# Four graph-attention layers on one core: buffer counts of three tiles, and the order and queues of the first loads

## The chip, the core and the metric

The kernel runs on one core of one Trainium2 chip. The core has a matrix engine (TensorE, PE in the profile), a vector engine (VectorE, DVE), an activation engine (ScalarE, ACT), a general engine (GpSimd, POOL), and SyncE (SP), which here only starts transfers. Each engine works through its own part of the program in the order written, and engines wait for one another on semaphores. Transfers are carried by 16 DMA engines that all issuers share. The metric is the time on the device in microseconds (us); the median over several executions is compared.

## What is computed

The input is 64 graphs ("groups" in the kernel) of 256 nodes with 256 features in float32, and for each an int32 adjacency matrix of 256 by 256. Four attention layers follow one another, each with a residual and a layer norm. The part around the change is the beginning of layer 0:

```python
q = proj(Wq, bq)
k = proj(Wk, bk)
v = proj(Wv, bv)
attn = jnp.einsum('bhnd,bhmd->bhnm', q, k) * scale
attn = jnp.where(adj[:, None, :, :] == 0, NEG, attn)
attn = jax.nn.softmax(attn, axis=-1)
out = jnp.einsum('bhnm,bhmd->bhnd', attn, v)
...
out = out @ Wo.T + bo
...
x = _layernorm(x + _L0_gnn_ref(...), axis=-1)
```

Layer 1 has eight heads whose queries, keys and values are the normed rows themselves, and an MLP of width 1024; layer 2 is additive attention; layer 3 is dot-product attention with edge types. All matrix products are float32.

## The kernel before

`usual_input` (lines 450 to 1171) writes out the program for all 64 groups. Each group is seven generators, called threads: `a` (load, mask, q, k, v, attention of layer 0), `u` (its normalization, output projection, norm), `z` (a transposition), `b` (attention of layer 1), `w`, `c` (MLP), `o` (the rest). Every `yield` ends a step. The order in which steps of different groups are written is laid down by hand: `FIRST` lists the first 657 steps as pairs of a thread letter and a group, `PLACES` gives the places within the steady period, `LAST` lists the end. The class `InOrder` (line 466) ties each engine's instructions to exactly this order; nothing is reordered later. Because every operation passes through it, nearly all lines of the profile carry its line, L475, and are told apart by tile names.

Steps that matter here, for a group g:

- `a`, step 0: `load_edges(g)` starts the transfer of the adjacency matrix into `adj` (2 buffers). Step 1 (line 720): ScalarE converts it to bfloat16, `adjb`, and squares it in place to check it. Step 2 (line 724): two transposing transfers on SP make `adjT` from `adjb`. Step 3: `load_x(g)`, four transfers into `turned` and one into `x` (for group 0 only the latter). Step 4: VectorE makes `xT`. Step 5 (line 741): VectorE makes `mask` from `adjT` and `adjb`; after it both are free. Then the matrix products for q, k, v and scores `ps`, the exponential `e` on ScalarE, its product with the mask on VectorE, sums `ea`, and the product of `e` with `v` on PE.
- `u` (line 806): VectorE takes the reciprocals of the softmax sums (`few`, `back`), then step 1 writes them to DRAM (`lines`), step 2 reads them back with two transfers, spread over 128 partitions, into `rr` (line 825), and step 3 (line 834) multiplies `oT` by `rr` on VectorE. After that `rr` is free. Step 4 is the product with `Wo`.
- `z`: `put` writes `z` to DRAM as `rows`, `get` reads it back as `blk`, VectorE turns it to `t`, ScalarE scales `t`, and the scores of layer 1 (`ps<-t` on PE) follow.

`BUFS` (line 46) gives the number of buffers of each tile name. When a tile has no free buffer, the first instruction that writes the next one waits until the last reader of the old one is done. Before the change `rr` has 2, `adjb` and `adjT` have 1 each.

At a few places in `FIRST` two groups are close together. Counting the steps of `FIRST` from 0, group 3's `rr` is read from DRAM at step 191 and used at 206; group 4's is read at 208 and used at 209. Group 2's `put` of `z` is step 220.

The weights' first loads are lines 570 to 578; the others are queued in `later` and started from SP step by step. `load` (line 537) takes the engine whose queue starts the transfer.

Of the kernel before, what the change touches and what calls it, by code (L numbers as in the profile page):

```python
# [18 lines left out]
D = 256  # L19
# [23 lines left out]
WARM = 2  # L43
XQ = True
DIRECT = {0: ('x', 'z', 'o', 'yT'), 63: ('yT', 'n2', 'n3', 'o')}
BUFS = {'t': 7, 'q': 3, 'k': 1, 'v': 3, 'y': 4, 'z': 4, 'xb': 4, 'both': 2, 'xn': 6, 'mask': 9, 'e': 7, 'x0': 3, 'turned': 2, 'blk': 4, 'oT': 3, 'zs': 1, 'rr': 2, 'xT': 1, 'qT': 1, 'kT': 1, 'adj': 2, 'adjb': 1, 'adjT': 1, 'hT': 2, 'ea': 3}
PLACES = {
# [402 lines left out]
def usual_input(ctx: ExitStack, tc: tile.TileContext, a: dict, out: bass.AP, flag: bass.AP):  # L450
# [34 lines left out]
    PE, DVE, ACT, POOL, SP = (InOrder(e) for e in (nc.tensor, nc.vector, nc.scalar, nc.gpsimd, nc.sync))  # L485
    matmul, transpose = PE.matmul, PE.transpose

    def new(pool, shape, dtype, name, bufs=None, tag=None):
        tag = tag or name
        if bufs is None:  # L490
            bufs = BUFS.get(tag)
        t = pool.tile(shape, dtype, name=name, tag=tag, **({} if bufs is None else dict(bufs=bufs)))
        return t
# [22 lines left out]
    def load_edges(g):  # L516
        adj = new(io, [P, TB, N], I32, "adj")
        SP.dma_start(adj, a["adj"][g].rearrange("(q p) k -> p q k", p=P))
        return adj

    def load_x(g):
        turned = None
        if FX and "x" not in DIRECT.get(g, ()):
            turned = new(io, [P, NC, N // 32, 32], F32, "turned")
            parts = a["x"][g].rearrange("(t i) (c k j) -> k i c t j", i=32, c=NC, j=32)
            for k in range(P // 32):
                if XQ:
                    SP.dma_start(turned[32 * k:32 * k + 32], parts[k])
                for c in range(0 if XQ else NC):
                    SP.dma_start(turned[32 * k:32 * k + 32, c], parts[k, :, c])  # L530
        x0 = new(io, [P, TB, D], F32, "x0")
        SP.dma_start(x0, a["x"][g].rearrange("(q p) d -> p q d", p=P))
        return x0, turned
# [3 lines left out]
    def load(queue, to, of):  # L537
        if queue:
            queue.dma_start(to, of)
        else:  # L540
            later[-1].append((to, of))

    def load_rows(name, cols, queue=None, parts=1):

        src = a[name]
        n = src.shape[0] // P
        t = const.tile([P, n, cols], F32, name=name)
        of = src.rearrange("(c p) f -> p c f", p=P)
        for k in range(parts):
            if k:  # L550
                later.append([])
            some = slice(k * n // parts, (k + 1) * n // parts)
            load(queue, t[:, some], of[:, some])
        return t

    def load_column(src, n, name, queue=None):

        t = const.tile([P, n // P], F32, name=name)
        load(queue, t, src.rearrange("(c p) -> p c", p=P))
        return t  # L560
# [3 lines left out]
    def load_all(src, name, at=None, queue=None):  # L564

        t = const.tile([P, D], F32, name=name) if at is None else setup[:, at:at + D]
        load(queue, t, src.unsqueeze(0).to_broadcast([P, D]))
        return t

    ACT.activation(few_out[:, 0:1], minus_half, AF.Exp)  # L570
    x_first = load_x(0)
    wqT = load_rows("L0_gnn_WqT", D, SP)
    wkT = load_rows("L0_gnn_WkT", D, SP)
    first = load_edges(0), x_first
    bq = load_column(a["L0_gnn_bq"], D, "bq", POOL)
    bk = load_column(a["L0_gnn_bk"], D, "bk", POOL)
    wvT = load_rows("L0_gnn_WvT", D, ACT)
    beta0 = load_all(a["L0_gnn_beta"], "beta0", queue=ACT)
    later.append([])
    woT = load_rows("L0_gnn_WoT", D)  # L580
    bv = load_column(a["L0_gnn_bv"], D, "bv")
# [592 lines left out]
@with_exitstack  # L1174
def four_layers(ctx: ExitStack, tc: tile.TileContext, a: dict, out: bass.AP):
    nc = tc.nc
    keep = ctx.enter_context(tc.tile_pool(name="keep", bufs=1))
    flag = keep.tile([1, 1], I32, name="flag")
    usual_input(tc, a, out, flag)
    unusual = nc.values_load(flag)  # L1180
    with tc.If(unusual > 0):
        any_input(tc, a, out)
# [25 lines left out]
```

## Time and profile before

| | us |
|---|---|
| median of 3 executions (2369.64 to 2371.6) | 2371.16 |
| the profiled execution, its own time | 2374.09 |
| span of its trace | 2372.3 |
| PE busy in that span | 2338.2 (99%) |
| VectorE busy | 1924.6 (81%) |
| ScalarE busy | 1819.8 (77%) |
| GpSimd busy | 686.9 (29%) |

All starts given below are microseconds from the start of the span. A timeline line has the start, the time taken, the engine, the instruction, what it writes and reads, how many of them stand in the row, and in brackets the idle time before with what ended it. "SPq", "ACTq" mean the issue of a transfer by that engine's queue, not the transfer itself. A line of the chain of waits has the start, the time and what the end of the kernel was waiting for in it. A window line has the stretch, its length, the busy time of PE, its clock as granted (1.00 is full speed), the share of the DMA engines' time that is busy, and the rate.

### The profile page before, as it was taken

To read this page: it belongs to the slowest core of one execution; us is meant where nothing else is said; L and a number is where in the kernel's file an instruction comes from. 1 tells how busy PE (TensorE), PEld (TensorE's weight loads), DVE (VectorE), ACT (ScalarE), POOL (GpSimd) and SP (SyncE) were. 2 spreads that over 40 slices of the span, in tenths; PEclk is the share of its full clock that TensorE was granted. 3 is DMA by queue.
4 is the path that set the end of the run, shared out by engine and by line. 5 is a ranking of instruction groups with operands and counts; after the bars stand their busy time and mean duration, and the time that the engine had idled before them with its cause. 6 is when DMAs were issued, how large, how long until landed. Compare 5 with 4: busy or idle time off the path is not lost.

```text
span 2372.3 us, 50135 instructions
## 1 busy us (share of the span) xinstructions
PE 2338.2 (99%) x16124; PEld 1882.1 (79%) x16124; DVE 1924.6 (81%) x6175; ACT 1819.8 (77%) x3976; POOL 686.9 (29%) x1742
## 2 busy tenths in 40 slices
PE   8999999999999999999999999999999999999997
PEld 5677788788788788788788887887887887877786
DVE  5898888888878878878888888888788788778764
ACT  5677877778787788788777777787877887777766
POOL 1122323322332332223223223223323232323232
PEclk9999999999999999999999999999999999999999
DMA  5455555555555555555555555555545545455442
GB/s 129 103 113 118 109 117 112 110 117 116 110 120 111 115 120 112 117 116 110 123 112 107 121 113 111 118 112 112 121 111 116 119 110 120 103 109 116 90 86 68
DMA packets 1088884, 265.08 MB, mean 112 GB/s; under 512 B 859364, under 2 KB 1088232, under 8 KB 1088616
## 3 DMA queue, kind: packets, MB, share of 16 engines
q1 hardware_dynamic: 1088136, 261.42, 51.3%
q8 instruction: 130, 2.13, 0.4%
q14 instruction: 138, 1.13, 0.2%
q10 hardware_dynamic: 416, 0.39, 0.1%
q0 software_dynamic: 64, 0.00, 0.0%
HBM read 153.37 MB, written 99.88 MB: 107 GB/s over the span
## 4 chain that ended last, share of the span: by engine, by line
PE 90%; DMA 3%; ACT 2%; DVE 2%; SPq 2%; issue 1%; POOL 1%; DVEq 0%; ACTq 0%; POOLq 0%
PE pm L475 80%; PE ps L475 10%; SPq L475 2%; DMA blk<-rows 1%; ACT xn L475 1%; DMA rows<-z 1%; DMA turned<-in_x 0%; ACT e L475 0%; DMA adj<-in_adj 0%; DVE y L475 0%; ACT z L475 0%; POOL rstd L475 0%; DMA rr<-lines 0%; DVE e L475 0%; DVE xT L475 0%
## 5 line engine op out<-in xcount | busy, mean ns | idle before, releaser
L475 DVE SCALAR_TENSOR_TENSOR e<-e,mask 128x256 f32<-128x256 f32 x1024 | 368.8, 420 | 210.9 <-ACT e L475 210.8
L475 PE MATMUL pm<-t,L_gnn_W 128*128 128x256 f32 x2048 | 459.7, 382 | 0.4 <-ACT oT L475 0.4
L475 PE MATMUL pm<-L_gnn_W,hT 128*128 128x256 f32 (+1 forms) x2064 | 455.0, 380 | 0.1
L475 PEld LDWEIGHTS pm<-t,L_gnn_W 128*128 128x128 f32 x2048 | 384.5, 190 | 67.4 <-issue 16.1
L475 PEld LDWEIGHTS pm<-L_gnn_W,hT 128*128 128x128 f32 (+1 forms) x2064 | 389.2, 189 | 54.6 <-issue 1.7
L475 ACT ACTIVATE e<-ps 128x1024 f32<-128x1024 f32 x384 | 381.1, 1018 | 51.4 <-PE ps L475 50.7
L475 POOL TENSOR_TENSOR rstd<-ve,mhalf 128x2 f32<-128x2 f32 (+1 forms) x384 | 314.4, 819 | 32.0
L475 POOL TENSOR_SCALAR ve<-sq 128x2 f32<-128x2 f32 x256 | 75.4, 294 | 798.1 <-ACT xn L475 526.8
L475 POOL TENSOR_SCALAR ve<-mv 128x2 f32<-128x2 f32 x192 | 48.1, 251 | 784.5 <-DVE rz L475 462.1
L475 DVE STREAM_TRANSPOSE t<-blk 128x512 f32<-128x512 f32 x313 | 219.6, 704 | 16.7 <-DMA blk<-rows 16.1
L475 ACT ACTIVATE hT<-pm,b 128x256 f32<-128x256 f32 x512 | 201.2, 474 | 17.3 <-PE pm L475 16.5
L475 ACT ACT_TABLE_LOAD x127 | 162.9, 1283 | 2.4 <-PEq L1194 0.7
L475 DVE TENSOR_TENSOR e<-e,mask 128x1024 f32<-128x1024 f32 x128 | 150.9, 1218 | 11.6 <-ACT e L475 11.5
L475 PE MATMUL ps<-t 32*128 32x256 f32 x2048 | 151.1, 404 | 5.2 <-ACT t L475 4.1
L475 ACT ACTIVATE xn<-y,nm,rstd 128x256 f32<-128x256 f32 x256 | 138.5, 593 | 11.0 <-POOL nm L475 9.0
L475 ACT ACTIVATE xn<-y,sums 128x256 f32<-128x256 f32 x256 | 126.6, 497 | 18.2 <-DVE y L475 18.0
L475 PEld LDWEIGHTS ps<-t 32*128 32x128 f32 x2048 | 95.5, 186 | 56.5 <-ACT oT L475 19.7
L475 ACT ACTIVATE few_out<-few 128x8 f32<-128x8 f32 x64 | 13.3, 208 | 162.2 <-DVE few L475 162.1
L475 POOL TENSOR_SCALAR nm<-nm 128x2 f32<-128x2 f32 x320 | 128.9, 403 | 28.0
L475 PE MATMUL pm<-xn,q 128*128 128x257 f32 x512 | 130.9, 381 | 3.5 <-ACT q L475 3.4
L475 DVE SCALAR_TENSOR_TENSOR y<-pm,r,xn 128x256 f32<-128x256 f32 x256 | 123.9, 484 | 9.6
L475 PE MATMUL pm<-e,v 128*32 128x256 f32 x2048 | 124.0, 383 | 5.0 <-DVE e L475 4.6
(149 smaller groups left out, 4646.0 us busy)
## 6 DMA issues: line engine op xcount, KB each, us to landing
blk<-rows SPq DMA_DIRECT2D x1252, 64.0 KB, 2.4
rows<-xn SPq DMA_DIRECT2D x252, 128.0 KB, 2.1
x<-in_x SPq DMA_DIRECT2D x64, 256.0 KB, 3.3
adj<-in_adj SPq DMA_DIRECT2D x64, 256.0 KB, 3.6
rr<-lines SPq DMA_DIRECT2D x128, 128.0 KB, 3.7
out<-xn SPq DMA_DIRECT2D x64, 256.0 KB, 2.5
turned<-in_x SPq DMA_DIRECT2D x252, 64.0 KB, 2.6
rows<-z SPq DMA_DIRECT2D x126, 128.0 KB, 1.9
```

Source lines behind the costliest of these rows:

```text
L475: ins = call(*args, **kw)
```

## The change

Three buffer counts change: `rr` goes from 2 to 1, `adjb` and `adjT` from 1 to 2. The memory per partition is the same: `rr` is 2 KB, the other two 1 KB each. And the first loads are written in another order and on other queues: the columns `bq` and `bk` are started by ScalarE, ahead of its first activation, and no longer by GpSimd; the first adjacency matrix is started ahead of `wkT`; `wvT` and `beta0` are started by SP, behind `wkT`, and no longer by ScalarE.

```diff
-BUFS = {... 'rr': 2, 'xT': 1, 'qT': 1, 'kT': 1, 'adj': 2, 'adjb': 1, 'adjT': 1, 'hT': 2, 'ea': 3}
+BUFS = {... 'rr': 1, 'xT': 1, 'qT': 1, 'kT': 1, 'adj': 2, 'adjb': 2, 'adjT': 2, 'hT': 2, 'ea': 3}
...
+    x_first = load_x(0)
+    bq = load_column(a["L0_gnn_bq"], D, "bq", ACT)
+    bk = load_column(a["L0_gnn_bk"], D, "bk", ACT)
     ACT.activation(few_out[:, 0:1], minus_half, AF.Exp)
-    x_first = load_x(0)
     wqT = load_rows("L0_gnn_WqT", D, SP)
+    first = load_edges(0), x_first
     wkT = load_rows("L0_gnn_WkT", D, SP)
-    first = load_edges(0), x_first
-    bq = load_column(a["L0_gnn_bq"], D, "bq", POOL)
-    bk = load_column(a["L0_gnn_bk"], D, "bk", POOL)
-    wvT = load_rows("L0_gnn_WvT", D, ACT)
-    beta0 = load_all(a["L0_gnn_beta"], "beta0", queue=ACT)
+    wvT = load_rows("L0_gnn_WvT", D, SP)
+    beta0 = load_all(a["L0_gnn_beta"], "beta0", queue=SP)
```

More of the change, by code (lines that the diff above doesn't have):

```diff
@@ L45 @@
 DIRECT = {0: ('x', 'z', 'o', 'yT'), 63: ('yT', 'n2', 'n3', 'o')}
-BUFS = {'t': 7, 'q': 3, 'k': 1, 'v': 3, 'y': 4, 'z': 4, 'xb': 4, 'both': 2, 'xn': 6, 'mask': 9, 'e': 7, 'x0': 3, 'turned': 2, 'blk': 4, 'oT': 3, 'zs': 1, 'rr': 2, 'xT': 1, 'qT': 1, 'kT': 1, 'adj': 2, 'adjb': 1, 'adjT': 1, 'hT': 2, 'ea': 3}
+BUFS = {'t': 7, 'q': 3, 'k': 1, 'v': 3, 'y': 4, 'z': 4, 'xb': 4, 'both': 2, 'xn': 6, 'mask': 9, 'e': 7, 'x0': 3, 'turned': 2, 'blk': 4, 'oT': 3, 'zs': 1, 'rr': 1, 'xT': 1, 'qT': 1, 'kT': 1, 'adj': 2, 'adjb': 2, 'adjT': 2, 'hT': 2, 'ea': 3}
 PLACES = {
```

## The prediction

> **What bounds the kernel now.** I read the page's busy table first, then windows over the span, then the waits of PE, the chain of waits, and last the timeline at the two places that the change touches.
>
> ```profile
> PE 2338.2 (99%) x16124; PEld 1882.1 (79%) x16124; DVE 1924.6 (81%) x6175; ACT 1819.8 (77%) x3976; POOL 686.9 (29%) x1742
> ```
>
> PE is idle for 2372.3 - 2338.2 = 34.1 us in all. Windows tell where: from 200 to 2000 it is idle for 0.6 us, up to 200 us for about 16, after 2000 us for 17. So nothing that the change does to the steady period can pay; one microsecond of PE idleness removed or added in the first 200 us moves the end by one microsecond, because behind it stand 1800 us without slack.
>
> At the start, from the timeline:
>
> ```profile
> 2.27 0.47 SPq L475 DMA_DIRECT2D adj<-in_adj  x1
> 8.34 0.63 ACT L475 ACTIVATE adjb<-adj 128x512 bf16<-128x512 int32 x1 [6.10 <-DMA adj<-in_adj]
> 9.09 2.58 SPq L475 DMA_TRANSPOSE adjT<-adjb  x2
> 13.69 0.63 ACT L475 ACTIVATE adjb<-adj 128x512 bf16<-128x512 int32 x1 [2.33 <-DVE mask L475]
> 14.44 2.46 SPq L475 DMA_TRANSPOSE adjT<-adjb  x2
> 15.63 1.94 ACT L475 ACTIVATE e<-ps 128x1024 f32<-128x1024 f32 x2
> 16.95 2.75 SPq L475 DMA_DIRECT2D turned<-in_x  x4
> 22.36 2.00 PE L475 MATMUL pm<-xT,L_gnn_WqT 128*128 128x256 f32 x8 [0.61 <-DVE xT L475]
> ```
>
> The first matrix lands 6.05 us after its issue. Group 1's conversion at 13.69 has waited 2.33 us for group 0's mask, which frees the only `adjb`; behind it on ScalarE stands the first exponential, behind it on SP the transposes and group 1's `turned`, on which PE's next products hang. The chain of waits runs through these same pieces up to about 70 us.
>
> The other place, from the timeline around 100 us:
>
> ```profile
> 97.59 1.29 SPq L475 DMA_DIRECT2D rr<-lines  x2
> 102.05 1.23 SPq L475 DMA_DIRECT2D rr<-lines  x2
> 103.37 1.05 SPq L475 DMA_DIRECT2D rows<-z  x2
> 106.81 0.68 DVE L475 TENSOR_TENSOR oT<-oT,rr 128x512 f32<-128x512 f32 x1
> 107.12 1.92 SPq L475 DMA_DIRECT2D blk<-rows  x4
> 108.30 0.67 DVE L475 TENSOR_TENSOR oT<-oT,rr 128x512 f32<-128x512 f32 x1
> ```
>
> Two `rr` are under way at once: group 4's is issued at 102.05, group 3's is used at 106.81. And the chain of waits goes through what follows on SP:
>
> ```profile
> 104.01 3.05 DMA rows<-z
> 108.55 3.83 DMA blk<-rows
> 112.50 0.72 DVE t L475
> 113.25 0.61 ACT t L475
> 113.91 1.15 PE ps L475 x16
> ```
>
> PE already waits 1.47 us for that last line, and then works nearly without a break.
>
> **What the Trainium skill says.** "DMA: Bandwidth & Descriptors", section on the anatomy of one DMA: a transfer's wait for a semaphore is held by the issuing sequencer before dispatch, not by the DMA engines. The trace agrees: ScalarE's row that writes `z` runs from 99.36 for 1.09 us, so `z` was complete at 100.45, yet `rows<-z` was issued at 103.37, right behind the waiting `rr`. The same page, "Issuing engines are not separate DMA queues": issuing from another engine saves only issue time, since all share the 16 DMA engines. In the trace those are 95 to 100% busy from 4 to 9 us, whoever issued. "TensorE: Matmul & The Clock Gate", Part 1: after an idle window of about 3.4 us PE falls to half clock, and one busy window brings it back; windows run free. The trace agrees in size:
>
> ```profile
> 17.50:18.00 0.50, 0.03 (x4) 0.50 0.47 87
> 20.50:21.00 0.50, 0.50 (x12) 0.60 0.80 126
> 66.00:67.00 1.00, 1.00 (x16) 0.50 0.16 31
> 75.00:76.00 1.00, 1.00 (x7) 0.75 1.05 342
> ```
>
> After 4.61 us of idleness the clock is 0.50 from about 17.5 to 20.7; after 2.28 us, itself preceded by little work, from 65.6 to 75.5.
>
> **The change, part by part.**
>
> *First loads.* On SP the order becomes x, wq, adj, wk, wv, beta0, about 0.5 us each: adj is issued at 1.75 and not 2.27, and with wv and beta0 behind it rather than beside it. By the fine windows the DMA engines had moved 0.88 MB when wq landed (5.2 us: x, wq and, on ScalarE's queue, wv stood before it), and some 1.7 MB when adj did, against 1.44 MB issued up to it. So a load lands when about 0.1 to 0.3 MB more than its queue position have moved. Adj's position is now 0.79 MB, so 1.0 MB, reached at about 5.7 us: 2.6 us earlier. Wk at 1.05 MB comes at 6.5 and is needed at 7.58; PE's 0.13 us of waiting for it goes. Wv at 1.31 MB comes at 7.7 and is needed at 9.5. Beta0 is needed after 12. The columns bq and bk cost two issues of 0.51 us on ScalarE's queue; its table load and first activation (1.5 us) end near 3.2, long before adj. They are needed at 7.6. GpSimd loses 1.66 us of issuing that nobody waited for.
>
> *SP's queue at the start.* Two more loads of 0.5 us stand on SP, and SP's issues also wait for old loads: its own waits show 0.4 us for wq and 2.0 us for wk ahead of the first transpose. I put `bo` and the second adj 1 to 1.5 us later than before (adj(1) at about 6.8, before 5.22), so the transposes of group 0 start at about 7.35, not 9.09: 1.75 us earlier; bounds 2.5 (right behind adjb at 6.6) and 0.5 (bk late, and SP waiting on it).
>
> *Two adjb, two adjT.* Group 1's conversion no longer needs the mask. It follows kT on ScalarE, at about 10.55 (PE's k product ends at 9.7, kT takes 0.84), if adj(1) has landed; before, that was at 11.0. Before: 13.69. The 2.33 us wait is gone; the exponential comes after conversion (0.75), square (0.73) and v (0.47) at 12.5, 3.1 us earlier. What is late next is SP. From the first transpose to group 1's it issued 2.58 + 0.53 + 4 x 0.49 us = 5.1 us, so these come at 7.35 + 5.1 = 12.5, not 14.44: 1.9 us. `turned`, `xT` and PE's next product shift by the same 1.9, and so does all that hangs on them up to 70 us. Sum of the start: -1.9 us, between -0.5 and -3.1. From there on only one more such wait exists (0.9 us, between 150 and 175, where PE does not wait).
>
> *One rr.* In the steady period `rr` is issued some 7 us before its use and the next one comes 29 us after that (1158.73, 1166.08, 1194.76), so one buffer is enough. I went through all 64: only at 102.05 is the next issue ahead of the use. There the issue must wait for the end of the multiplication, 106.81 + 0.68 = 107.49. Behind it on SP stand `rows<-z`, `blk<-rows`, the transposes of group 6 and the rest. SP is held for 107.49 - 102.05 = 5.4 us. `rows<-z` goes to 108.8, `blk<-rows` to 112.5, landing at 117.9, `t` on VectorE and ScalarE, and PE's scores at 119.3 in place of 113.91. VectorE waits too: the fourth group's multiplication can start when its `rr` has landed, about 4.35 us after the issue (25.18 to 29.5 in the first group), at 111.9, not 108.30; but that lies inside the other delay, and so do PE's 8 products behind it (1.9 us). PE had no other work in this gap, since its order is fixed. So +5.4 us at PE, and nothing behind takes it back. Bounds: 4.5, if group 4's lines come 0.9 us later than now; 6, if the rows' transfer finds the engines busier.
>
> *Clock.* PE is then idle for about 2 us and, after the 1.9 us of products, nearly 5 us. By the two cases above the clock falls. At least about 2.8 us of work at half speed follow, as at 17.97 to 20.7: 1.4 us lost; at most, as at 65.6 to 75.5 with 9 us of work, 4.5 us; 0 if it doesn't fall. I take 1.6.
>
> Sum: -1.9 + 5.4 + 1.6 = +5.1 us. The profiled execution, 2374.09 us (span 2372.3, and 1.8 around it), becomes 2379.2; it stood 2.9 over the median, so the median of 2371.16 becomes 2376.3, 0.2% slower.
>
> **Rivals.**
>
> *The wait does not reach PE (not slower; 0.23).* Place: SP at 102.05. It decides if VectorE finishes the earlier multiplication before group 4's `lines` have landed, that is 5.4 us sooner relative to SP, or if SP gets there that much later. Against it: VectorE takes that multiplication behind two mask products (103.33 to 105.7) and the sums that hang on ScalarE's exponential at 102.30. For it: the head runs shifted, and loads stand elsewhere. Then only the start counts: 2371.2 - 1.9 = 2369.3; if the earlier start also spares the slow clock from 65.6 on, worth up to 4.5, 2364.8.
>
> *The clock stays down for three windows (slower; 0.13).* As at 65.6, because scores with gaps follow a stall. -1.9 + 5.4 + 4.5 = +8: 2379.2. Against it: behind 119 us stand full products of the MLP.
>
> *The start gains nothing (0.06).* ScalarE's small columns are slow to land (bv took 6.1 us, bq from GpSimd 5.7), SP waits on them before `bo` and the second adj, and that lands after 12. Then +5.4 + 1.6 = +7: 2378.2.
>
> **How the numbers follow.** The forecast has 0.58. A measurement of this kernel tells about 0.2%, 4.7 us, from no change; the forecast's own range is +2 to +8, of which I put 0.42 above that bound and 0.16 below. The second rival is slower (0.13), the third nearly always (0.05 and 0.01 same), the first is faster in 0.15, same in 0.08. Faster 0.15, same 0.25, slower 0.60. For 8 in 10 I leave out the lower part of the first rival and the top of the second: 2367 to 2380.5; the forecast's own is 2373 to 2379.
>
> **What would show it.** In the trace after: no wait of `adjb` for the mask, group 1's transposes near 12.5, PE's second group near 20.5; near 100 us a wait of SP for VectorE's `oT` of about 5.4 us, the two multiplications some 5 us apart and not 1.5, and a PE gap of about 5 us ahead of `ps<-t`, with a clock of 0.50 behind it. I am wrong if SP issues the two `rr` as close as now, or if PE is idle for less in the first 130 us than it was.

## The result and the profile after

| | before | after |
|---|---|---|
| median of 6 executions, us | 2371.38 | 2381.05 |
| lowest to highest, us | 2369.64 to 2372.86 | 2377.57 to 2383.92 |
| the profiled execution, us | 2374.09 | 2381.22 |
| span of its trace, us | 2372.3 | 2379.4 |

The ratio is 1.0037, with a 95% interval from 1.0027 to 1.0048: the change makes the kernel slower by 9.7 us. The direction is the one forecast; the size is about twice as large (+5.1 us) and lies above the forecast's own range of +2 to +8 us. The busy table of the page of the kernel after:

```profile
PE 2339.5 (98%) x16124; PEld 1880.8 (79%) x16124; DVE 1924.1 (81%) x6175; ACT 1821.3 (77%) x3976; POOL 686.8 (29%) x1740
```

PE does the same work, 1.3 us longer in sum; its idle time has grown from 34.1 to 39.9 us. To find where, I laid the 64 multiplications of `oT` by `rr` side by side in the two traces. Group 3's comes 1.82 us later than before, group 4's 5.51, group 5's 9.76; from group 7 to group 59, over 1800 us, the distance is 9.8 to 9.9 us without change. So nearly everything that the change does, it does before 150 us. (After 2100 us the profiled execution of before loses about 2.8 us on that of after, half of it in 16 products that take 4.47 us there and 2.98 here, its clock being 0.78 after 2350 us. So these two spans differ by 7.1 us, the medians by 9.7.)

The start, from the timeline of the kernel after, in the same columns as before:

```profile
1.74 0.47 SPq L475 DMA_DIRECT2D adj<-in_adj  x1
7.21 0.63 ACT L475 ACTIVATE adjb<-adj 128x512 bf16<-128x512 int32 x1 [3.92 <-DMA adj<-in_adj]
7.96 2.59 SPq L475 DMA_TRANSPOSE adjT<-adjb  x2
11.13 0.63 ACT L475 ACTIVATE adjb<-adj 128x512 bf16<-128x512 int32 x1 [0.18 <-DMA adj<-in_adj]
13.07 1.94 ACT L475 ACTIVATE e<-ps 128x1024 f32<-128x1024 f32 x2
13.25 2.46 SPq L475 DMA_TRANSPOSE adjT<-adjb  x2
15.76 2.74 SPq L475 DMA_DIRECT2D turned<-in_x  x4
22.55 3.78 PE L475 MATMUL pm<-xT,L_gnn_WqT 128*128 128x256 f32 x8 [4.19 <-DVE xT L475]
```

The wait of `adjb` for the mask is gone and the exponential runs 2.56 us earlier, as intended. But PE's next group does not profit: it starts at 22.55 (before 22.36), after a gap of 4.19 us, and its eight products take 3.78 us in place of 2.00.

The place near 100 us, timeline of the kernel after:

```profile
98.96 1.30 SPq L475 DMA_DIRECT2D rr<-lines  x2
108.63 0.68 DVE L475 TENSOR_TENSOR oT<-oT,rr 128x512 f32<-128x512 f32 x1
109.34 1.23 SPq L475 DMA_DIRECT2D rr<-lines  x2
110.66 1.05 SPq L475 DMA_DIRECT2D rows<-z  x2
113.81 0.69 DVE L475 TENSOR_TENSOR oT<-oT,rr 128x512 f32<-128x512 f32 x1 [3.62 <-DMA rr<-lines]
114.59 3.09 SPq L475 DMA_DIRECT2D blk<-rows  x4
```

Group 4's `rr` is now issued at 109.34, 0.03 us after group 3's multiplication ends (108.63 + 0.68); before, it was issued while that multiplication was still 4.8 us away. `rows<-z`, which has nothing to do with `rr`, comes behind it. The chain of waits of the kernel after carries this on to PE:

```profile
111.30 3.23 DMA rows<-z
...
116.02 3.36 DMA blk<-rows
119.41 0.72 DVE t L475
120.15 0.61 ACT t L475
120.81 2.09 PE ps L475 x16
```

The scores start at 120.81 and not 113.91: 6.90 us later, of which 1.81 were there already when PE began the product of `e` with `v` before it (108.23, before 106.42). They also take 2.09 us, not 1.15. The lines of PE that this rests on, first those of the kernel before, then those of the kernel after:

```profile
106.42 1.93 PE L475 MATMUL pm<-e,v 128*32 128x256 f32 x32 [0.21 <-ACT hT L475]
118.63 1.15 PE L475 MATMUL ps<-t 32*128 32x256 f32 x16
...
108.23 1.93 PE L475 MATMUL pm<-e,v 128*32 128x256 f32 x32 [0.33 <-ACT hT L475]
128.55 1.15 PE L475 MATMUL ps<-t 32*128 32x256 f32 x16
```

Windows of PE in the kernel after (stretch, length, PE busy, clock, share and rate of the DMA engines):

```profile
112.00:116.00 4.00, 1.88 (x9) 1.00 0.42 112
116.00:120.00 4.00, 0.61 (x3) 1.00 0.41 68
120.00:123.00 3.00, 2.19 (x17) 0.54 0.41 109
123.00:126.00 3.00, 3.00 (x8) 0.50 0.53 85
126.00:129.00 3.00, 3.00 (x18) 0.82 0.47 74
```

PE stands nearly still from 112 to 120 and then works at half clock until about 127. The next scores, at 118.63 before, start at 128.55: 9.92 us later. Between these two executions, then: 1.8 us from the start, 5.1 from the wait, 3.0 from the clock. The first two parts lean on the one trace of the kernel before; what other traces say of them stands in the account of the prediction and in the last section.

### The profile page after: what moved, and what is told of

Its sections match the earlier page's. It is cut to its first block, busy times and chain, and to the rows that moved or that the text cites. A ratio compares the mean times of both kernels' runs of the same rounds, so it can differ in the third digit from the quotient of the medians.

```text
span 2379.4 us, 50132 instructions
## 1 busy us (share of the span) xinstructions
PE 2339.5 (98%) x16124; PEld 1880.8 (79%) x16124; DVE 1924.1 (81%) x6175; ACT 1821.3 (77%) x3976; POOL 686.8 (29%) x1740
## 4 chain that ended last, share of the span: by engine, by line
PE 89%; ACT 3%; DMA 3%; DVE 2%; SPq 1%; POOL 1%; issue 1%; DVEq 0%; ACTq 0%; POOLq 0%
PE pm L475 79%; PE ps L475 10%; SPq L475 1%; DMA blk<-rows 1%; ACT xn L475 1%; POOL rstd L475 0%; DVE e L475 0%; DVE y L475 0%; ACT e L475 0%; ACT z L475 0%; DVE t L475 0%; DMA adj<-in_adj 0%; DMA turned<-in_x 0%; ACT hT L475 0%; DVE q L475 0%
## 5 line engine op out<-in xcount | busy, mean ns | idle before, releaser
L475 PE MATMUL pm<-xT,L_gnn_WqT 128*128 128x256 f32 x512 | 123.5, 385 | 5.8 <-DVE xT L475 4.5
```

The source lines that it names most:

```text
L475: ins = call(*args, **kw)
```

## The experiments

Theory: the wait for the one `rr` buffer, in front of other groups' transfers in SP's queue, is the cause, with half clock behind it. Rivals: the loads' new order, or the second `adjb` or `adjT`, or something in PE's products. All ratios are to the kernel before, timed on the same chip beside each, and a gain or loss in us is taken from the ratio where one is given. Where the three buffers should all be 2, the memory of the core does not suffice; `adjT` then stays at 1; its buffer is free before group 1's transposes are due (in e4_after_rr2 the mask that reads it is done at 12.03, the transposes begin at 12.83).

### One part at a time

**e1_rr1**: the kernel before with `'rr': 1`.

```diff
-'rr': 2
+'rr': 1
```

> The kernel before with one buffer of rr and nothing else. Theory (the wait for the earlier multiplication holds SP near 100 us): the trace up to 97 us is that of the kernel before; the two multiplications of oT by rr lie about 5 us apart in place of 1.5; the scores behind them start about 5.1 us later (some 119 in place of 113.91), and half clock behind the gap costs 1.5 to 3 us more: 6.5 to 8 us over the kernel before, about 2378.5. Rival (the loss comes from the first loads or from the new buffers): within 1.5 us of the kernel before.

Measured: 2379.84 us, ratio 1.0039 (1.0026 to 1.0053), so 9.2 us slower. PE's timeline:

```profile
113.25 1.97 PE L475 MATMUL pm<-L_gnn_WoT,oT 128*128 128x256 f32 x8 [2.10 <-DVE oT L475]
120.04 2.09 PE L475 MATMUL ps<-t 32*128 32x256 f32 x16 [4.82 <-ACT t L475]
122.06 5.89 PE L475 MATMUL pm<-L_gnn_W,hT 128*128 128x256 f32 x16
127.88 1.15 PE L475 MATMUL ps<-t 32*128 32x256 f32 x16
```

This alone reproduces the whole loss. Group 3's multiplication is 0.45 us later than in the kernel before (107.26), the scores 6.13, the next scores 9.25: 5.7 us of wait and 3.1 of clock. It is a little over what was expected.

**e2_adjb2**: the kernel before with two `adjb`.

```diff
-'adjb': 1
+'adjb': 2
```

> The kernel before with two buffers of adjb alone (adjT stays at 1, rr at 2, since all three do not fit in memory; adjT's single buffer is free at 13.65, before group 1's transposes are ready to start). Theory: group 1's conversion no longer waits 2.33 us for the mask, the first exponential comes 2 to 3 us earlier, but SP is still busy with its loads to 14.3, so PE's second group stays near 22.3 and the time is within 1.5 us of the kernel before. Rival (the conversion's wait is what sets the start): 2 to 3 us faster. Second rival (a second buffer lets ScalarE's work collide with the exponential): slower by over 1 us.

Measured: 2373.06 us, ratio 1.0012 (1.0005 to 1.0018). The size is that of the second rival: the buffer that removes a wait of 2.33 us makes the kernel slower by 2.8 us. The collision on ScalarE that this rival named is not seen: in the trace the first exponential starts at 14.84, 0.79 us earlier than before.

**e3_loads**: the new order and queues of the loads, all buffer counts as before.

```diff
-'rr': 1, ... 'adjb': 2, 'adjT': 2
+'rr': 2, ... 'adjb': 1, 'adjT': 1
```

(against the kernel after). 

> The new order and queues of the first loads with the old buffer counts. Theory (wq lands later by 0.8 us, the transfer of group 1's turned lands late and PE falls to half clock in the gap): 1 to 3 us slower than before, wq near 6.3, PE's second group at 22 to 23 followed by a half-clock stretch. Rival (the earlier adjacency matrix pays): 1 to 3 us faster.

Measured: 2368.17 us, ratio 0.9990 (0.9983 to 0.9997). My theory at that point, read off the one trace of the kernel after, was wrong: the loads alone gain 2.4 us. PE's second group begins at 20.82 in its trace, 1.5 us before that of the kernel before.

**e4_after_rr2**: the kernel after with `rr` at 2 (and `adjT` at 1).

```diff
-'rr': 1, ... 'adjT': 2
+'rr': 2, ... 'adjT': 1
```

> The kernel after with two buffers of rr again (adjT back at 1 to make room, adjb at 2). Theory: the 5 us gap ahead of the scores near 114 is gone and with it the half clock behind it; what is left is the start, 0 to 3 us over the kernel before: 2371.5 to 2374. Rival (rr is not the cause): it stays at 2378 to 2382 like the kernel after.

Measured: 2370.58 us, ratio 1.0001 (0.9992 to 1.0009). PE's timeline:

```profile
22.15 2.83 PE L475 MATMUL pm<-xT,L_gnn_WqT 128*128 128x256 f32 x8 [3.88 <-DVE xT L475]
...
105.97 1.93 PE L475 MATMUL pm<-e,v 128*32 128x256 f32 x32 [0.19 <-ACT hT L475]
...
108.26 3.72 PE L475 MATMUL pm<-L_gnn_WoT,oT 128*128 128x256 f32 x16
112.31 1.15 PE L475 MATMUL ps<-t 32*128 32x256 f32 x16 [0.33 <-ACT t L475]
113.38 3.72 PE L475 MATMUL pm<-L_gnn_W,hT 128*128 128x256 f32 x16
```

The gap is down to 0.33 us, and the products behind it run at full clock. The parts add up: the loads' -2.4 us and the second `adjb`'s +2.8 leave nothing. `rr` is the loss. For the second `adjT`, which no run has alone, this leaves -0.7 us (the kernel after less e1_rr1 and e4_after_rr2), less than the intervals resolve.

### What the wait consists of

**e5_mul_early**: in the kernel after, group 3's multiplication is written ahead of group 5's mask products (place 206 of `FIRST` moved to 199; each entry is a thread and a group).

```diff
-a6 w1 a5 a5 a5 c0 c0 c0 c0 u3 w1 u4 u4
+a6 w1 u3 a5 a5 a5 c0 c0 c0 c0 w1 u4 u4
```

> The kernel after, with group 3's multiplication of oT by rr written seven steps earlier, ahead of group 5's mask products (FIRST, from place 206 to 199); rr keeps its one buffer. Theory (SP is held until VectorE has done this multiplication, which stands behind some 3.6 us of mask products and sums): SP issues group 4's rr about 1.5 to 2 us later than with two buffers and not 5.4 to 7, the scores near 114 are hardly late, no half clock follows: 2370 to 2373, that is 8 to 11 us under the kernel after. Rival (one buffer costs time in other ways than this one wait): stays above 2376.

Measured: 2375.13 us, ratio 1.0021 (1.0015 to 1.0028); better than after, and between the numbers of theory and rival. The timeline (`FIRST` takes a line less here, so the lines read L474):

```profile
102.50 0.68 DVE L474 TENSOR_TENSOR oT<-oT,rr 128x512 f32<-128x512 f32 x1
103.21 1.23 SPq L474 DMA_DIRECT2D rr<-lines  x2
104.53 1.05 SPq L474 DMA_DIRECT2D rows<-z  x2
...
114.42 1.66 PE L474 MATMUL ps<-t 32*128 32x256 f32 x16 [2.66 <-ACT t L474]
```

SP's issue follows the multiplication here too, 0.03 us behind its end. With PE at the product of `e` with `v` 0.23 us before that of e4_after_rr2 (105.74 and 105.97), `rows<-z` is still 2.4 us later than there (104.53 and 102.08) and the scores 2.1 us. I had counted on 1.5 to 2 us and no half clock; PE's gap of 2.66 us was enough for it: the scores and the 16 products behind them take 1.66 and 4.85 us, not 1.15 and 3.72.

**e11_put_first**: e5_mul_early with group 2's `put` of `z` (place 220) written ahead of group 4's read of `rr` (208).

```diff
-w1 u4 u4 c0 c0 c0 c0 w1 a5 u3 u4 a5 u5 z2 z2 z2
+w1 z2 u4 u4 c0 c0 c0 c0 w1 a5 u3 u4 a5 u5 z2 z2
```

> e5_mul_early (one rr, group 3's multiplication earlier) with group 2's put of z written ahead of group 4's read of rr, so that it does not stand behind the wait. Theory (one rr costs only what is queued behind its wait on SP): no gap over 0.5 us ahead of the scores near 112, no half clock there, and about the time of e4_after_rr2, ratio 0.9995 to 1.0006. Rival (group 4's late rr or VectorE's changed order costs by itself): ratio over 1.0015, as in e5_mul_early (1.0021).

Measured: 2371.52 us, ratio 1.0004 (0.9998 to 1.0011). Its timeline:

```profile
101.44 0.89 SPq L474 DMA_DIRECT2D rows<-z  x2
104.62 0.69 DVE L474 TENSOR_TENSOR oT<-oT,rr 128x512 f32<-128x512 f32 x1
105.33 1.23 SPq L474 DMA_DIRECT2D rr<-lines  x2
...
114.27 1.15 PE L474 MATMUL ps<-t 32*128 32x256 f32 x16 [0.38 <-ACT t L474]
```

`rr` has one buffer and its issue still waits for the multiplication, but nothing urgent stands behind it. The gap is 0.38 us and the loss is gone. (The scores stand at 114.27 and not at 112.31 as in e4_after_rr2 because PE was 1.9 us later already at the product of `e` with `v`, 107.87 and 105.97; from there to the scores it is 6.40 and 6.34 us.) So it is not the buffer count as such, but what is queued behind the wait. One thing stays open: here the late `rr` of group 4 keeps neither VectorE nor PE waiting, since the multiplication ahead of it was moved too. In the kernel after PE stood 2.12 us for group 4's `oT`; whether moving `rows<-z` alone would have been enough there, no run shows.

**e6_filled_gap**: the kernel after with four products of ones by ones on PE behind group 4's product with `Wo`. It does more than the kernel after; nothing reads these products.

```diff
+        if g == 4:
+            busy = new(ps_m, [P, QB * N], F32, "pm", 4)
+            for _ in range(4):
+                matmul(busy..., ones, ones..., start=True, stop=True)
```

> The kernel after, with four products of ones by ones (128x512 each, some 3.7 us at full clock) written on PE behind group 4's product with Wo, that is into the gap of 4 to 5 us ahead of the scores. Their output is not used. Theory (of the 9 us that one rr costs, about 3 are the half clock behind the gap): no half clock behind 120 us, 2 to 3 us less than the kernel after, about 2378.5. Rival (the products behind the gap are slow for another reason, their operands): the same time as the kernel after or more.

Measured: 2378.42 us, ratio 1.0036 (1.0023 to 1.0050); after is at 1.0037. The medians differ by 2.6 us, the ratios hardly, since the kernel before was 1.7 us faster beside this run; by the time alone this is not settled. The trace is clear. Windows of PE, to be held against those of the kernel after:

```profile
120.00:123.00 3.00, 2.45 (x22) 1.00 0.33 93
123.00:126.00 3.00, 3.00 (x23) 1.00 0.59 93
```

Full clock, and the scores (1.15 us) and the products behind (3.72) as fast as before the change. From the scores' start to the next scores' start it is 4.73 us here, 7.74 in the kernel after: 3.0 us of half clock, and the operands of those products are not the reason.

### The start

**e7_filled_start**: e4_after_rr2 with three products of ones by ones behind group 0's sums; their output is not used.

```diff
+        if g == 0:
+            busy = new(ps_m, [P, QB * N], F32, "pm", 4)
+            for _ in range(3):
+                matmul(busy..., ones, ones..., start=True, stop=True)
```

> The kernel with the new loads, two adjb and two rr (e4_after_rr2), with three products of ones by ones written on PE behind group 0's sums, into the gap of 3 to 4 us ahead of group 1's q product. Their output is not used. Theory (a second adjb moves PE's gap from ahead of group 0's products with v, which VectorE paces, to ahead of group 1's projections, which PE paces, and the half clock with it): group 1's q and k take 2.0 and 1.9 us and not 2.8, 1.5 to 2.5 us less than e4_after_rr2, about 2368.5. Rival (adjb's second buffer costs elsewhere): no change, 2370 to 2371.

Measured: 2369.38 us, ratio 0.9998 (0.9990 to 1.0007). The line that answers to the first of e4_after_rr2, from PE's timeline:

```profile
22.12 1.99 PE L475 MATMUL pm<-xT,L_gnn_WqT 128*128 128x256 f32 x8 [1.33 <-DVE xT L475]
```

The half clock is gone at this place, as expected, but the ratio falls only by 0.0003, which cannot be told from nothing.

**e9_adjb2_filled**: the same with two such products in e2_adjb2.

```diff
-            for _ in range(3):
+            for _ in range(2):
```

> The kernel before with two adjb (e2_adjb2) and two products of ones by ones on PE behind group 0's sums (1.9 us, in the gap of some 2 us ahead of group 1's q product; their output is not used). Theory (what the second adjb costs in the median, some 2.4 us, is half clock behind a gap that now lies ahead of group 1's projections): back to the time of the kernel before, ratio 0.999 to 1.0004. Rival (the cost lies elsewhere): ratio stays near 1.0012.

Measured: 2370.68 us, ratio 1.0003 (0.9995 to 1.0012), where e2_adjb2 had 1.0012. It goes the way of the theory, but the intervals overlap, and in the trace of e2_adjb2, the fastest of its executions, group 1's q product runs at full clock (1.99 us). That the second `adjb` costs through the clock is not shown.

**e8_x_first**: e4_after_rr2 with the loads of `gamma0`, `beta1r`, `gamma1` and `beta1` (place 18) behind group 1's `turned` and `x` (23).

```diff
-l0 a1 a0 a0 a0 a1
+a1 a0 a0 a0 a1 l0
```

> e4_after_rr2 with the four loads of gamma0, beta1r, gamma1 and beta1 written behind group 1's turned and x instead of ahead of its transposes (FIRST, place 18 to behind place 23). Theory (with a free adjb it is SP's queue that is late next): group 1's transposes start 1 to 1.5 us earlier, PE's second group near 20.5 and not 22.2, the gap ahead of it is 2 us shorter: 2 to 3.5 us less than e4_after_rr2, 2367 to 2368.5. Rival (turned is late because of the transfers in flight, not of its issue): within 1 us of e4_after_rr2.

Measured: 2369.57 us, ratio 0.9999 (0.9990 to 1.0007). PE's second group does start at 20.65 and not 22.15, but SP's queue accounts for only 0.67 us of that (`turned` is issued at 14.67, not 15.34). The rest is that `turned` lands sooner behind its issue, so theory and rival each have a share. And a new wait of 1.63 us for group 0's `oT` comes behind it, at 30.52, and at the scores near 112 only 0.7 us are left (111.63 and 112.31).

**e10_loads_x_first**: the same move in e3_loads.

```diff
-l0 a1 a0 a0 a0 a1
+a1 a0 a0 a0 a1 l0
```

> The new loads with the old buffers (e3_loads), with the four loads of gamma0, beta1r, gamma1 and beta1 behind group 1's turned and x. Theory (SP's queue between the two pairs of transposes sets the start): PE's second group some 0.5 to 1 us earlier than e3_loads, since the one adjb still holds the conversion until the mask; ratio 0.998 to 0.999. Rival (the gain of an earlier second group is lost again before 70 us): the same as e3_loads, 0.999, or more.

Measured: 2367.70 us, ratio 0.9991 (0.9983 to 1.0000), the rival's number: no more than e3_loads. Its second group started at 21.57, so the step that was to come earlier did not in its trace, and the move was not put to the test by it. Both are faster than before and after; e3_loads, which keeps the old buffers, is the version to take, as its interval excludes no change.

**What the traces add on the second `adjb`.** It moves nothing on SP. The two pairs of transposes begin 5.35 us apart with one buffer (before) and 5.37 us with two (e2_adjb2); with the new loads it is 5.36 (e3_loads) and 5.37 (e4_after_rr2), since SP's own issues fill that time. Behind the same issues, `turned` lands later. The lines of e3_loads, with one `adjb`:

```profile
12.87 2.46 SPq L475 DMA_TRANSPOSE adjT<-adjb  x2
15.38 2.74 SPq L475 DMA_DIRECT2D turned<-in_x  x4
20.05 0.71 DVE L475 STREAM_TRANSPOSE xT<-turned 128x512 f32<-128x512 f32 x1 [1.37 <-DMA turned<-in_x]
```

and of e4_after_rr2, with two; the last line is from its DMA queues between 15.34 and 21.38 (packets, MB, share of the DMA engines' time):

```profile
12.83 2.46 SPq L475 DMA_TRANSPOSE adjT<-adjb  x2
15.34 2.74 SPq L475 DMA_DIRECT2D turned<-in_x  x4
21.38 0.71 DVE L475 STREAM_TRANSPOSE xT<-turned 128x512 f32<-128x512 f32 x1 [3.80 <-DMA turned<-in_x]
...
q8 instruction: 1, 0.02, 1.1%
```

From the first issue of `turned` to `xT` it is 4.65 to 4.83 us in before, e1_rr1 and e3_loads, all with one `adjb`, and 5.90 to 6.08 us in seven of the nine traces with two. All nine have a packet of the queue that the profile names "instruction" in that stretch, and none of the four with one `adjb` has it. The exceptions are e8_x_first (two, 5.21 us), e2_adjb2 (two, 4.74 us, with the packet in its last 0.4 us) and e10_loads_x_first (one, 5.37 us). That this packet delays `turned`, and that this is what the second `adjb` costs, fits the traces, but no run tested it.

## Why the prediction was right in direction and short in size

- **One `rr`, the wait.** Right in place, mechanism and nearly in size. Forecast: SP held for 5.4 us, scores 5.4 us late. Measured: 5.1 us in the trace of after, 5.7 in that of e1_rr1, both against the one trace of before. In that trace it takes 7.49 us from the start of the product of `e` with `v` to the scores, but 6.34 in each of the seven other traces with two `rr` (the kernel before has no second trace, so what is usual for it is not known). Against those the wait costs 6.2 us (after, 12.58) and 6.8 (e1_rr1, 13.18), so the term was somewhat too small. That nothing else on PE takes it back is shown by the constant 9.8 to 9.9 us from group 7 on. VectorE's own wait (3.62 us for group 4's `rr`) lay inside, as said. e11_put_first shows that the queue behind the wait is the cause, not the buffer count as such.
- **Clock behind the gap.** Right that it falls, mis-sized: the term was 1.6 us, taken near the short one of two cases; it measured 3.0 (after) and 3.1 (e1_rr1). (The short case ended at 20.9, not 20.7: a mean clock of 0.60 from 20.5 to 21.0 is half clock for 0.4 us.) PE's busy stretch at half clock was some 6 us, between the 2.8 and 9 us that bounded it. With the wait, one `rr` costs 9.2 us by e1_rr1, where the prediction had 7.0.
- **The start.** This is the step that failed: -1.9 us were forecast, about none were there (e4_after_rr2: 1.0001, -2 to +2 us). The sum treated the loads and the second `adjb` as one chain whose end moves by what SP gains. Taken apart they have opposite signs, -2.4 and +2.8 us. The -1.9 is what the loads alone give: in e3_loads group 1's transposes begin at 12.87 and PE's second group at 20.82 (forecast 12.5 and 20.5). What failed is that the second `adjb`, which has no part in this, was given no price: it costs 2.8 us (e2_adjb2), or 2.6 (e4_after_rr2 against e3_loads). Step by step in the trace of after: the second matrix was issued at 6.82 (forecast 6.8), the first transposes began at 7.96 (7.35), group 1's at 13.25 (12.5), both late because the first matrix landed at 7.2 and not 5.7. The last piece of `turned` then took 3.83 us after its issue, before 2.41, and PE's second group started at 22.55, not 20.5. Here the prediction moved the landing with the issue and did not ask whether it would.
- **What the start's sum left out.** Ahead of group 0's products with `v` and ahead of group 1's q product, PE's gaps were 4.61 and 0.61 us before and are 1.68 and 4.19 us after: the earlier exponential shortened the first, and the second grew, since `turned` did not land sooner. In the trace of after the clock falls in the second, and group 1's q and k products take 6.6 us, not 3.9. Before, half clock fell on group 0's products with `v` (3.35 us, after 2.21), behind which PE still had 0.61 us to wait. The prediction put a price on the clock near 112 us and none here. Whether the second `adjb` costs its 2.6 to 2.8 us in the median through the clock, through the late `turned`, or both, stays open: e7_filled_start and e9_adjb2_filled moved the time less than they can resolve, and `turned` landed late in both.
- **The rivals.** The one that kept the wait from PE did not come. That the clock stays down longer came halfway. That the start gains nothing did come, but not through the small columns: SP waited 0.8 us for `bq` and 1.0 us for `bk` ahead of its next loads, yet e3_loads, with the same columns, is faster than before.

## What to carry to other kernels

In this kernel a buffer count is a wait in the queue of whoever writes the tile first; ask at every place where two uses overlap what else stands in that queue, since one place in 64 was enough here. If memory must be found, first move what frees the buffer forward and the urgent instruction ahead of the wait, as e11_put_first does, then give the buffer up. Parts of a change that act on the same stretch should be tried one at a time: two edits that together look neutral were a gain and a loss.

## What the runs showed that I had not expected

- A gap of 2.66 us on PE (e5_mul_early), shorter than the idle window of about 3.4 us that the prediction names, can be enough for half clock to follow, with 1.6 us lost in the 32 products behind it; after 4.2 to 4.8 us it was 3.0 to 3.1 us. In e6_filled_gap, where only a gap of 0.83 us was left, nothing was lost. The length of one gap does not decide it: e3_loads has one of 3.01 us, ahead of 16.39, and the clock from 15 to 25 us stays at 1.00.
- The new loads start slowly, but after 10 us as much has been moved as before: in the first 5 us the transfers run at 91 GB/s (after), 101 (e3_loads) and 103 (e4_after_rr2), where they ran at 166 before; in the next 5 us at 329, 329 and 327, against 243.
- Single traces mislead on effects of 2 us: e3_loads gains where the trace of after spoke of a loss, and the profiled execution of e2_adjb2, 2369.77 us, is the fastest of its 21, while their median is 2373.06. Nor does the 1.8 us that the trace of after has lost by 108 us belong to the new start as such. Five kernels have that start (e4_after_rr2 with one `adjT` buffer): e4_after_rr2 and e5_mul_early begin the product of `e` with `v` at 105.97 and 105.74, with a mean clock of 0.94 from 10 to 100 us; e11_put_first, e6_filled_gap and after at 107.87, 108.21 and 108.23, with 0.92.
